# Six context tiles' values as three pairs of seven block products, with their sums on VectorE

## The chip, the cores and the metric

The kernel runs as one program on one core of one Trainium2 chip. The metric is the device time of one execution in microseconds (us). A core has a matrix engine (TensorE, "PE" in the profile, whose weight loads are "PEld"), VectorE ("DVE"), ScalarE ("ACT"), GpSimd ("POOL") and a queue engine (SyncE, "SP"), each with its own instruction stream; they wait for each other by semaphores. Matrix products read SBUF, the on-chip memory of 128 partitions, and are written to PSUM, eight banks of 2 KB a partition, here one tile of 128x512 float32 each.

## The reference, cut to what matters

Two layers work on a residual x of 2 x 256 tokens and 512 features. The first has an attention-like product with quantised factors and a mixture of experts; the second has a cross attention to 2 x 512 context rows, and then a low-rank layer with a gate. The cross attention, as the reference has it:

```python
q = (hidden_states @ q_proj_w.T).reshape(B, Q, NUM_HEADS, HEAD_DIM).transpose(0, 2, 1, 3)
k = (cross_attention_states @ k_proj_w.T).reshape(B, KV, NUM_KV_HEADS, HEAD_DIM)...
v = (cross_attention_states @ v_proj_w.T).reshape(B, KV, NUM_KV_HEADS, HEAD_DIM)...
q = rmsnorm(q, q_norm_w); k = rmsnorm(k, k_norm_w)
scores = einsum('bhqd,bhkd->bhqk', q, k) * scale + attention_mask
attn = softmax(scores); out = einsum('bhqk,bhkd->bhqd', attn, v)
return out @ o_proj_w.T
```

There are 32 query heads, 8 key and value heads ("groups" here, four query heads to each) and 128 features a head. The values of all groups are a matrix of 1024 context rows (8 tiles of 128) by 1024 columns, made from the context (512 features) and a weight matrix of 512 by 1024. The change is about the second half of its columns, groups 4 to 7.

## The kernel before, in words

All matrix products of this stage are float32. The values' first half is made at the start of the kernel. The second half is made at the start of the attention, by `values` (L723): for a context tile m, `context_product` (L216) multiplies four chunks of 128 features of the context, already transposed (`cT1`), with the weights `wv1` into one PSUM bank by four products of 128x512, and ACT copies the bank into `vv[:, m, 512:]` (L727).

The stage's order is written out at the end of the function, from L1100: layer norms of the four token tiles (L1103) and value tiles 0 and 1, the tokens turned (L1106), queries of group 0 for tiles 0 and 1, value tiles 2 and 3 (L1111), queries of tiles 2 and 3; then scores of unit (0, 0) two heads at a time (`probs`, L852) with a value tile behind each pair of heads: tiles 4, 5, 6, 7 at L1131, L1133, L1135, L1139. The first query products of group 1 stand between value tile 6 and the next scores (L1136). From L1141 a loop runs over units (group, token tile); it makes scores two units ahead, attends (`pav`), and makes queries and output products.

`in_order[0] = True` (L1101) holds PE's products and POOL's sums in the order in which the program writes them. DVE and ACT have no such order: the framework's planner places their instructions, each in one stream that runs strictly in order, and adds the semaphores. `tc.issue_after(x)` lets what is written inside be placed behind x.

Two other products of the stage already have a seven-product form (a product of 2x2 blocks by seven block products and sums of blocks, in the variant of Winograd). In `queries_begun` (L809) four block products of two steps of 128x256 are written into two banks `pe` and `po`; ACT copies one quarter to `u2`, and DVE forms three dependent adds (L824, L826, L827). In `queries_ended` (L830) three more block products accumulate into or overwrite quarters of the same banks, and DVE adds `u2` twice (L837, L838). The tiles `u2` and `u3` are in a pool with one buffer (`usum`, L718). Each query tile is normalised: ACT squares it (L735), DVE reduces it (L741, L743), POOL takes the root (L185), DVE multiplies (L748) and transposes blocks into `zq` (L231, one buffer), and 16 transfers turn `zq` into `qT` (L239), which the scores read. For groups after the first these transfers are issued by POOL.

A score tile (L863) lies in one of three PSUM buffers (`psa`). DVE adds the mask and finds the minimum (L871), ACT exponentiates (L876), DVE inverts the sum (L878), ACT scales (L879), DVE transposes blocks into `z` (L231), and SP moves `z` to `pT`.

`bank_of` (L74) hands out PSUM buffers from a list of pools in turn; the list `turns_b` is set by hand from stage to stage. `oT`, `zT`, the sums of heads (`head_sums`, L931) and the `shared` accumulators have SBUF buffers from the stage's start; two memsets on POOL clear `shared` (L1129).

## Time and profile before

Three runs took 636.58 us in the median (635.55 to 638.62). The profiled execution took 636.27 us, of which 634.5 us is the span between its first and its last recorded instruction.

| What | Value |
|---|---|
| profiled execution | 636.27 us, span 634.5 us |
| mean granted clock of TensorE | 0.997 |
| PE busy | 620.6 us, 98% of the span, 2013 instructions |
| DVE busy | 461.8 us, 73%, 1174 |
| ACT busy | 285.0 us, 45%, 567 |
| POOL busy | 302.1 us, 48%, 453 |
| value products of the second half (tiles 2 to 7) on PE | six tiles of 3.43 us each |
| ACT copy of a value tile (L727) | 0.58 us |

How to read it: a row of a timeline has the start in us, the length, the engine, the line of the kernel, the operation, output and input by the program's names, partitions and shapes, and the number of records merged; in brackets the idle time of the engine just before, and what ended it. PE records one float32 product as two records. The length of a merged PE row includes the draining of its last record, so the next row may start before it ends. DVE's instructions too are recorded with a small overlap. The granted clock is the share of full speed that the throttle let PE have.

### The profile page before, as it was taken

The page shows a single profiled execution, that of the slowest core. Times are in us where ns is not written, and L with a number is a line of the kernel's source. Part 1 is how long each engine was busy: PE and PEld are TensorE (multiplying, and loading weights), DVE is VectorE, ACT ScalarE, POOL GpSimd, SP SyncE. Part 2 cuts the span into 40 slices and gives each one's busy share as a digit, 9 for nine tenths or more (in the row PEclk, how much of TensorE's full clock was granted, in tenths as well). Part 3 has the DMA queues.
Part 4 walks back from the last instruction along what each step waited for, and adds up shares of the span by engine and source line. Part 5 has one row for each costly group of instructions (what it writes and reads, how often), then busy time and mean ns, then how long its engine had stood idle before and what let it go on. Part 6 is the DMA issues. An engine that isn't in the chain of part 4 may idle for free.

```text
span 634.5 us, 7774 instructions
## 1 busy us (share of the span) xinstructions
PE 620.6 (98%) x2013; PEld 395.9 (62%) x2013; DVE 461.8 (73%) x1174; ACT 285.0 (45%) x567; POOL 302.1 (48%) x453
## 2 busy tenths in 40 slices
PE   5999999999999999999999999999999999999997
PEld 2455345764456657776777767776677776665554
DVE  2568977765375888797887877878779788886533
ACT  0762132321165555555456545655555644644110
POOL 2308425301475772962844566467285346842200
PEclk9998999999999999999999999999999999999999
DMA  8740047450145754474474465457348446532101
GB/s 288 257 141 0 5 104 256 96 203 2 54 150 141 213 142 100 120 236 103 106 217 119 97 193 146 98 143 208 78 119 234 98 112 197 155 103 56 54 18 50
DMA packets 51950, 82.74 MB, mean 130 GB/s; under 512 B 15584, under 2 KB 17392, under 8 KB 51008
## 3 DMA queue, kind: packets, MB, share of 16 engines
q1 hardware_dynamic: 31232, 49.63, 28.3%
q10 hardware_dynamic: 11088, 19.41, 9.7%
q0 software_dynamic: 9584, 13.18, 7.7%
q8 instruction: 17, 0.28, 0.2%
q14 instruction: 29, 0.24, 0.1%
HBM read 34.97 MB, written 1.05 MB: 57 GB/s over the span
## 4 chain that ended last, share of the span: by engine, by line
PE 64%; DVE 0%; issue 0%; POOL 0%
PE pav L564 16%; PE px L564 16%; PE ps L564 15%; PE pq L564 11%; PE pz L564 2%; PE pout L564 2%; PE psc L564 1%; PE pzT L212 0%; PE pxn L212 0%; DVE qn L748 0%; DVE ot L1055 0%; POOL qrs L185 0%
## 5 line engine op out<-in xcount | busy, mean ns | idle before, releaser
L239 POOL DMA_DIRECT2D qT<-zq x232 | 114.4, 502 | 49.5 <-PE pav L564 32.3
L876 ACT ACTIVATE s<-s,nm 128x512 f32<-128x512 f32 x128 | 92.3, 721 | 75.4 <-DVE nm L871 69.3
L564 PE MATMUL ps<-kT,qT 128*128 128x512 f32 x256 | 121.0, 596 | 0.2 <-issue 0.2
L564 PE MATMUL pav<-pT,vv 128*128 128x512 f32 x256 | 115.3, 592 | 0.3 <-ACT s L879 0.3
L879 ACT ACTIVATE s<-s,rs 128x512 f32<-128x512 f32 x128 | 86.0, 710 | 55.2 <-DVE rs L878 42.6
L871 DVE CUSTOM_DVE_ANT_0 s<-ps,maskt 128x512 f32<-128x512 f32 x128 | 87.0, 681 | 24.1 <-PE ps L564 24.0
L231 DVE STREAM_TRANSPOSE z<-s 128x512 f32<-128x512 f32 x128 | 86.0, 697 | 14.6 <-ACT s L879 12.7
L564 PEld LDWEIGHTS ps<-kT,qT 128*128 128x128 f32 x256 | 77.9, 317 | 28.1 <-issue 4.5
L185 POOL TENSOR_TENSOR qrs<-qss,nhalf 128x4 f32<-128x4 f32 x32 | 32.3, 1015 | 103.9 <-DVE rs L878 59.4
L564 PEld LDWEIGHTS pav<-pT,vv 128*128 128x128 f32 x256 | 48.5, 190 | 49.9 <-issue 47.1
L221 PE MATMUL pk<-wk,cT 128*128 128x512 f32 x128 | 58.3, 611 | 1.1 <-DVE kn L291 1.1
L564 PE MATMUL pq<-wq,xnT 128*128 128x256 f32 (+1 forms) x200 | 57.4, 414 | 1.3 <-DVE qn L748 1.3
L564 PE MATMUL px<-wo,oT 128*128 128x256 f32 (+1 forms) x200 | 57.2, 413 | 0.0
L564 PEld LDWEIGHTS pq<-wq,xnT 128*128 128x128 f32 x200 | 37.7, 190 | 22.6 <-issue 16.1
L564 PEld LDWEIGHTS px<-wo,oT 128*128 128x128 f32 x200 | 37.8, 190 | 19.1 <-issue 12.7
L221 PEld LDWEIGHTS pk<-wk,cT 128*128 128x128 f32 x128 | 24.3, 195 | 30.2 <-issue 27.2
L221 PE MATMUL pv<-wv,cT 128*128 128x512 f32 x96 | 43.0, 593 | 0.2 <-PEq L689 0.2
L185 POOL TENSOR_TENSOR rs<-ve,nhalf 128x1 f32<-128x1 f32 x16 | 10.0, 629 | 64.5 <-DVE ve L196 50.0
L906 ACT COPY oT<-pav 128x512 f32<-128x512 f32 x32 | 18.4, 575 | 49.5 <-PE pav L564 49.5
L239 POOL DMA_DIRECT2D pT<-z x48 | 23.6, 499 | 32.9 <-issue 27.5
L878 DVE RECIPROCAL rs<-sm 128x1 f32<-128x1 f32 x128 | 19.4, 158 | 23.4 <-ACT s L876 22.1
L748 DVE TENSOR_TENSOR qn<-pq,qrs 128x512 f32<-128x512 f32 x32 | 22.1, 692 | 15.4 <-POOL qrs L185 15.4
(260 smaller groups left out, 937.1 us busy)
## 6 DMA issues: line engine op xcount, KB each, us to landing
pT<-z SPq DMA_DIRECT2D x464, 64.0 KB, 2.1
wo<-in_wqo_dram ACTq DMA_DIRECT2D x32, 256.0 KB, 3.9
qT<-zq POOLq DMA_DIRECT2D x232, 32.0 KB, 2.0
wq<-in_wqo_dram ACTq DMA_DIRECT2D x28, 256.0 KB, 3.9
kT<-vv SPq DMA_DIRECT2D x64, 64.0 KB, 2.0
cT<-in_cxT_dram SPq DMA_DIRECT2D x3, 1024.0 KB, 7.2
pT<-z POOLq DMA_DIRECT2D x48, 64.0 KB, 2.5
ct<-in_cx_dram SPq DMA_DIRECT2D x8, 256.0 KB, 4.7
```

Source lines behind the costliest of these rows:

```text
L185: last_root[0] = in_place(nc.gpsimd.tensor_tensor(dst, src, nhalf[:, :n], ALU.pow))
L221: last_product[0] = nc.tensor.matmul(ps, lhsT=c[:, kc, st * P : (st + 1) * P], rhs=w[:, kc, :], start=(kc == 0), stop=(kc == KC - 1),)
L231: nc.vector.transpose(z, src)
L239: ins = e.dma_start(dst[w * 32 : (w + 1) * 32, a], z[a * 32 : (a + 1) * 32, w])
L564: return in_place(nc.tensor.matmul(*args, **kw))
L748: nc.vector.tensor_tensor(qn, pq.rearrange("p (h d) -> p h d", d=HD), rq.unsqueeze(2).to_broadcast([P, REP, HD]), ALU.mult,)
L871: nc.vector.tensor_tensor_reduce(out=s, in0=sps, in1=maskt[:, mt, :], scale=-1.0, scalar=BIG, op0=ALU.add, op1=ALU.min, accum_out=nm,)
L876: nc.scalar.activation(s, s, AF.Exp, bias=nm, scale=-1.0, accum_out=sm)
L878: nc.vector.reciprocal(rs, sm)
L879: nc.scalar.mul(s, s, rs)
L906: nc.scalar.copy(oT.rearrange("p h a j -> p a h j"), po.rearrange("p (a h j) -> p a h j", a=NQ, h=REP),)
```

## The change

Value tiles 2 to 7 are made as pairs (2, 3), (4, 5), (6, 7). Each pair is a product of 256 context rows, 512 features and 512 columns. It is split into 2x2 blocks and made by seven block products of two steps of 128x256 each, in place of eight products of 128x512. Tiles 0 and 1 stay as they were.

- `value_weight_sums` forms four sums of blocks of `wv1` once, 128x512 each, and `value_sums` four sums of blocks of `cT1` for each pair, 128x256 each. All are DVE instructions. Some blocks are overwritten in place. Those of the weights and of pair 2 are written behind the last layer norm; those of pairs 4 and 6 behind the last add of pair 2.
- `values_begun` makes four of the seven products in two banks, has ACT copy a quarter to `u2` and DVE form three adds, the last into `vv`. `values_ended` makes the other three; ACT copies one quarter to `vv` and DVE adds twice into `vv`. `u2` and `u3` come from the pool `usum` with one buffer, by the tags that the queries use.
- In the order, `values_begun(2)` and `values_ended(2)` stand around the query product of tile 2. `values_begun(4)` and `values_ended(4)` stand where tiles 4 and 5 stood. `values_begun(6)` stands where tile 6 stood and `values_ended(6)` where tile 7 stood.
- The new sums have SBUF buffers in a pool at the right end of memory (`vsump`), closed behind `values_ended(6)`. The buffers of `oT`, `zT`, the heads' sums and `shared` are opened there then (`late`), and POOL's two memsets of `shared` move to that place.
- The list of PSUM buffers that the values use is set anew.

```diff
-        nc.vector.tensor_scalar(dst, src, mv[:, 0:1], rs, ALU.subtract, ALU.mult)
+        last_norm[0] = nc.vector.tensor_scalar(dst, src, mv[:, 0:1], rs, ALU.subtract, ALU.mult)
...
+        def value_weight_sums():
+            w = wv1.rearrange("p (i k) (j n) -> p i j k n", i=2, j=2)
+            b11, b12, b21, b22 = w[:, 0, 0], w[:, 0, 1], w[:, 1, 0], w[:, 1, 1]
+            t2, t3, t4 = (
+                vsump.tile([P, 2, 256], FP, tag=f"t{j}", bufs=1, name=f"vt{j}") for j in (2, 3, 4)
+            )
+            nc.vector.tensor_tensor(t3, b22, b12, ALU.subtract)
+            nc.vector.tensor_tensor(b12, b12, b11, ALU.subtract)
+            nc.vector.tensor_tensor(t2, b22, b12, ALU.subtract)
+            nc.vector.tensor_tensor(t4, b21, t2, ALU.subtract)
+            return b11, b21, b22, b12, t2, t3, t4
+
+        def value_sums(m):
+            b, st = divmod(m, S2 // P)
+            a = cT1[b].rearrange("p (i k) (s q) -> p i s k q", i=2, q=P)
+            a11, a12, a21, a22 = a[:, 0, st], a[:, 1, st], a[:, 0, st + 1], a[:, 1, st + 1]
+            s2, s3, s4 = (vsump.tile([P, 2, P], FP, tag=f"s{j}", name=f"vs{j}_{m}") for j in (2, 3, 4))
+            nc.vector.tensor_tensor(s3, a11, a21, ALU.subtract)
+            nc.vector.tensor_tensor(a21, a21, a22, ALU.add)
+            nc.vector.tensor_tensor(s2, a21, a11, ALU.subtract)
+            nc.vector.tensor_tensor(s4, a12, s2, ALU.subtract)
+            vsum_of[m] = a11, a12, a22, a21, s2, s3, s4
+
+        def values_begun(m):
+            a11, a12, a22, s1, s2, s3, s4 = vsum_of[m]
+            b11, b21, b22, t1, t2, t3, t4 = vsum_of["w"]
+            pe, po = (bank_of(turns_b, [P, 2, 256], FP, f"pv1_{m + o}") for o in range(2))
+            of_e = block_product(pe[:, 0], a11, b11, True)
+            of_o = block_product(po[:, 1], s2, t2, True)
+            with tc.issue_after(of_o):
+                block_product(po[:, 0], s3, t3)
+            with tc.issue_after(of_e):
+                block_product(pe[:, 1], s1, t1)
+            u2 = usum.tile([P, 256], FP, tag="u2", name=f"vu2_{m}")
+            nc.scalar.copy(u2, pe[:, 0])
+            nc.vector.tensor_tensor(u2, u2, po[:, 1], ALU.add)
+            u3 = usum.tile([P, 256], FP, tag="u3", name=f"vu3_{m}")
+            nc.vector.tensor_tensor(u3, u2, po[:, 0], ALU.add)
+            nc.vector.tensor_tensor(vv[:, m + 1, 768:], u3, pe[:, 1], ALU.add)
+            vpair_of[m] = pe, po, u2
+
+        def values_ended(m):
+            a11, a12, a22, s1, s2, s3, s4 = vsum_of.pop(m)
+            b11, b21, b22, t1, t2, t3, t4 = vsum_of["w"]
+            pe, po, u2 = vpair_of.pop(m)
+            block_product(pe[:, 0], a12, b21)
+            block_product(po[:, 0], a22, t4)
+            block_product(pe[:, 1], s4, b22)
+            nc.scalar.copy(vv[:, m, 512:768], pe[:, 0])
+            nc.vector.tensor_tensor(vv[:, m + 1, 512:768], u2, po[:, 0], ALU.add)
+            vpair_done[0] = nc.vector.tensor_tensor(vv[:, m, 768:], u2, pe[:, 1], ALU.add)
...
         for t in range(NT):
             turned(2, t)
-        turns_b[:] = [pso, pso, psb]
+        turns_b[:] = [pso]
         hold_loads[0] = True
+        with tc.issue_after(last_norm[0].ins):
+            vsum_of["w"] = value_weight_sums()
+            value_sums(2)
         next_queries(0)
         next_queries(1)
-        values((2, 3))
+        values_begun(2)
         next_queries(2)
         load_parts(4)
+        values_ended(2)
+        with tc.issue_after(vpair_done[0].ins):
+            value_sums(4)
+            value_sums(6)
...
-        for b in range(B):
-            nc.gpsimd.memset(shared[b], 0.0)
         probs(*units[0], (0, 1))
-        values((4,))
+        values_begun(4)
         probs(*units[0], (2, 3))
-        values((5,))
+        values_ended(4)
         probs(*units[1], (0, 1))
-        values((6,))
+        turns_b[:] = [psb, pso]
+        values_begun(6)
         next_queries(4)
         probs(*units[1], (2, 3))
+        values_ended(6)
         turns_b[:] = [pso]
-        values((7,))
+        vsums.close()
+        late.append(att.enter_context(tc.tile_pool(name="late", bufs=3, side="right")))
+        for b in range(B):
+            shared.append(late[0].tile([P, 2, 256], FP, tag=f"shared{b}", bufs=1, name=f"shared{b}"))
+            nc.gpsimd.memset(shared[b], 0.0)
```

More of the change, by code (lines that the diff above doesn't have):

```diff
@@ L188, in pool_sum @@
         in_place(nc.gpsimd.tensor_tensor(dst, a, b, op))
+    last_norm = [None]
     def layernorm(dst, src):
@@ L711, in tile_fq_moe_xattn_lora @@
         qtp = att.enter_context(tc.tile_pool(name="qtp", bufs=2))
-        opool = att.enter_context(tc.tile_pool(name="opool", bufs=3))
         spool = att.enter_context(tc.tile_pool(name="spool", bufs=4))
@@ L718, in tile_fq_moe_xattn_lora @@
         usum = att.enter_context(tc.tile_pool(name="usum", bufs=1))
+        vsums = ExitStack()
+        vsump = vsums.enter_context(tc.tile_pool(name="vsump", bufs=2, side="right"))
         norm_pool[:] = spool, "s"
@@ L729, in normed_queries @@
+        vsum_of, vpair_of, vpair_done = {}, {}, [None]
         def normed_queries(g, tiles, pqs):
@@ L904, in attend @@
             pT_of.pop((g, t))
-            oT = opool.tile([P, REP, NQ, 32], FP, tag="oT", name=f"oT{g}_{t}")
+            oT = late[0].tile([P, REP, NQ, 32], FP, tag="oT", name=f"oT{g}_{t}")
             nc.scalar.copy(
@@ L921, in project @@
             nc.vector.tensor_add(xs[t], xs[t], px)
-        shared = [
-            wsump.tile([P, 2, 256], FP, tag=f"shared{b}", name=f"shared{b}") for b in range(B)
-        ]
+        shared, late = [], []
         def head_sums(g, b):
@@ L934, in head_sums @@
             s2, s3, s4 = (
-                wsump.tile([P, 2, P], FP, tag=f"o{j}", name=f"o{j}_{g}_{b}") for j in (2, 3, 4)
+                late[0].tile([P, 2, P], FP, tag=f"o{j}", bufs=1, name=f"o{j}_{g}_{b}") for j in (2, 3, 4)
             )
@@ L1019, in gated_turned @@
         def gated_turned(t):
-            zT = opool.tile([P, KC, P], FP, tag="oT", name=f"zT{t}")
+            zT = late[0].tile([P, KC, P], FP, tag="oT", name=f"zT{t}")
             transposed(zT, f_of.pop(t).rearrange("p e r -> p (e r)"), f"pzT{t}")
```

## The prediction

> **What bounds the kernel now.** I read the page first, then the chain that ended last, then PE's waits, then the rows of PE, DVE, ACT and POOL from 150 to 232 us, where the change lies, and last the granted clock by windows. The first fence is the page (engine totals) and the chain's shares.

> ```profile
> PE 620.6 (98%) x2013; PEld 395.9 (62%) x2013; DVE 461.8 (73%) x1174; ACT 285.0 (45%) x567; POOL 302.1 (48%) x453
> PE 64%; DVE 0%; issue 0%; POOL 0%
> ```

> PE is the bound over the whole span; the chain is PE alone from 226 us to the end. So a PE slot removed is time removed, and a PE wait added is time added. PE's rows in the stage (start, length with drain, operation):

> ```profile
> 161.91 7.03 PE L221 MATMUL pv<-wv,cT 128*128 128x512 f32 x16
> 168.77 7.03 PE L564 MATMUL pq<-wq,xnT 128*128 128x512 f32 x16
> 175.64 1.88 PE L564 MATMUL ps<-kT,qT 128*128 128x512 f32 x4
> 177.36 3.60 PE L221 MATMUL pv<-wv,cT 128*128 128x512 f32 x8
> ...
> 191.09 1.03 PE L564 MATMUL pq<-wq,xnT 128*128 128x256 f32 x4
> 191.95 1.89 PE L564 MATMUL pq<-qt,xsum 128*128 128x256 f32 x8
> 193.68 1.03 PE L564 MATMUL pq<-wq,xnT 128*128 128x256 f32 x4
> ...
> 201.43 1.03 PE L564 MATMUL pq<-wq,xnT 128*128 128x256 f32 x4
> ```

> From 161.91 to 209 no row of PE shows a wait. The reader is to see two prices: a pair of value tiles takes 168.77 - 161.91 = 6.86 us, and the queries' products already have the new form: four block products 191.09 to 194.54 = 3.45, three 201.43 to 204.02 = 2.59. PE's waits of the span, in part:

> ```profile
> PE pv L309 <- DMA wv<-in_wkv_dram: 7.1, 1, 7.1
> PE pq L564 <- DVE qn L748: 1.3, 1, 1.3
> ```

> The 1.3 us stand at 226.36; behind that PE never stops for more than 0.3. Now DVE's rows where the new work goes:

> ```profile
> 183.32 1.30 DVE L231 STREAM_TRANSPOSE z<-s 128x512 f32<-128x512 f32 x2
> ...
> 195.15 0.42 DVE L824 TENSOR_TENSOR u<-u,pq 128x256 f32<-128x256 f32 x1 [3.77 <-ACT u L823]
> ...
> 229.63 0.40 DVE L937 TENSOR_TENSOR o<-oT,oT 128x256 f32<-128x256 f32 x1
> ```

> From 177.37 on DVE serves masks, transposes and normalisations with gaps of 0.1 to 0.8 us only. Last, the clock (columns: window; PE, PEld, DVE, ACT, POOL busy; PEclk; DMA share; GB/s):

> ```profile
> 52.40:55.90 3.50, 3.50 (x28) 3.02 (x27) 2.19 (x8) 1.57 (x7) 3.50 (x3) 1.00 0.00 0
> 55.90:59.30 3.40, 3.40 (x6) 1.49 (x6) 3.37 (x9) 0.89 (x3) 3.24 (x4) 0.50 0.00 0
> 59.30:62.70 3.40, 3.40 (x9) 1.52 (x8) 3.37 (x9) 0.47 (x1) 3.24 (x6) 1.00 0.00 0
> ```

> In the first window PE has mostly 16-column records and only two full ones of 128x512; then the clock is 0.50 for 3.4 us.

> **The change part by part.** Times are those of this trace.

> *PE, removed.* Three pairs at 3.45 + 2.59 = 6.04 instead of 6.86: 3 x 0.82 = 2.46 us less.

> *DVE, added.* Four sums of weights (128x512, pitch 0.61 by L748) and four of tiles 2, 3 (128x256; the head sums L937, L938 start 0.32 apart between SBUF operands): 2.4 + 1.3 = 3.8 us, placed behind the last layer norm, which ends at 153.96. They end near 157.8; DVE's next own work is the reduction at 159.35, and PE wants the sums at 162.8. Nothing. Eight more sums for tiles 4 to 7: 8 x 0.33 = 2.6 us. Five adds a pair, 15 in all; three of each pair form a dependent chain at 0.45 a step (195.15 to 195.60).

> *ACT.* Six copies of 128x512 (0.58) become six of 128x256 (0.37): nothing, ACT is 45% busy and waits for PE before most of them.

> *The new wait, first pair (2, 3).* The old products ended in one ACT copy and PE never waited. Now the second three products of a pair overwrite a bank that DVE must have read in its third add. Pair 2: first products end 165.4, the adds run behind the transpose at 165.7 and end 167.9; PE is on a query tile until 168.8. No wait.

> *Second pair (4, 5).* PE: three products end 171.4, query tile 174.8, two scores 176.5, four products 180.0, two scores 181.7. Then it wants DVE's third add. DVE's queue in the built order of the changed kernel: the query's product at 171.8 (square, reduction and POOL's root of 1.02 in front, 3.4 us before their old place), an add, 172.7; the transpose must wait for the reads of the same buffer by the transfers issued until 172 and landing 2.0 later, about 173.2; 0.95, an add 0.33, then the eight sums: 177.1. A reduction 0.61, mask 0.68, 0.08, mask 0.68: 179.1. The wait for POOL's root, as before (178.72 to 179.25): 179.6. Product 0.72, transpose 0.95, two masks with reciprocals 1.52, two transposes 1.26: 184.1. Three adds: 185.4. PE waits 185.4 - 181.7 = **3.7 us**. Everything on PE queues behind that wait: the tile's end, the next scores, and so their masks.

> *Third pair (6, 7).* Between its halves stand four query products and two scores, so its own adds (194.9 done) are early. But the query half-products use the same single-buffered "u2" tile: the ACT copy that stood at 194.74 must wait until DVE has read the values' u2 for the last time. PE: 185.4 + 2.6 + 1.7 + 3.5 + 3.45 + 1.7 = 198.4, three products to 201.0, two scores to 202.7; it then wants the query pair's third add. DVE's last value add ends 202.4 (behind two transposes), the copy 202.8, two masks are in front until 203.7, three adds: 205.0. PE waits **2.3 us**, where it waited nothing before.

> *What is late next.* At this point (201.43 before) PE stands at 205.1: 3.6 to 3.7 late = 3.7 + 2.3 - 2.4. From here a chain sets the wait at 226.36: the query tiles' products, POOL's 16 transfers (212.62 to 220.50), three sums, two roots, DVE's product. It shifts with PE. The small waits at 209.2 and 216.6 (0.1 and 0.3 us) vanish and the one at 226.36 grows by some 0.4, DVE having fewer leftovers in between: net **+3.3 us**.

> *POOL.* The two memsets (0.99) move from 139.95 behind the third pair, about 201; POOL is idle there from 198.8 to 207.4: nothing. SP's queue has the same transfers in the same order; ACT's loads of weights start up to 1.7 earlier or 2 us later, and are read at 220.5 by POOL: nothing.

> *The clock.* PE's 226.36 gap of 1.27 us left the clock at 1.00 (windows after it); the stretch before 55.90, with some 0.9 us of full records in 3.4, dropped it to 0.50 for 3.42 us; and after 7.07 us idle at the start records take 1061 ns instead of 592. A wait of 3.7 us is nearest to the second row: I take one drop, 3.42 / 2 = **+1.7 us**; bounds 0 and two drops, 3.4.

> [...]

> [...]

> **Sum.** The profiled execution took 636.27 us (span 634.5 and 1.8 around it); the median of the three runs shown is 636.58, 0.3 above. 636.27 + 3.3 + 1.7 = **641.3 us**.

> Unknowns: the sums of 128x256 at 0.33 each, up to 0.42 if their starts don't overlap (+0.7 on eight); the landing of the query transfers, 2.0 median and 3.7 at most in the trace (+1.7 on the first wait, since ACT's weight loads now start while they run); DVE 5% quicker than my rows would take 0.6 off. So without the clock +2.6 to +4.3 on most counts.

> **Rivals.**
> 1. *The clock stays at 1.00.* For it: the gap at 226.36 cost no clock. Against: that gap was a third as long. 636.27 + 3.3 = 639.6.
> 2. *Two drops.* Behind the 2.3 us wait too, or the first wait is a us or more longer by a late landing. For it: the stretch before 55.90 was not even idle. Against: 2.3 of 3.4 us leaves a third of a window busy. 636.27 + 3.3 + 3.4 = 643.0, with the landing 644.
> 3. *The waits are covered (other side).* If DVE reached the third add of the second pair by 181.7 and the u2 copy by 199, only the removed products would show: 636.27 - 2.46 = 633.8. The place is the eight sums and two transposes ahead of the add; it decides once DVE is there 3.7 us sooner, the sum of all eight sums and one and a half transposes. Against it: DVE has no gap from 173.2 to 179.1 in the built order and none from 179.6 to 185.4. Break-even needs both waits together under 2.5.

> **How the numbers follow.** One drop 0.52 (own range 640.3 to 642.5), no drop 0.27 (638.8 to 640.5), two drops or late landing 0.14 (642.5 to 644.8), covered waits in part or whole 0.07 (633.8 to 638.8). The range from 638.8 to 644.3 leaves out the last case and the end of the third. 0.5%, 3.2 us, is about what a measurement of this kernel can tell from no change: from 633.4 to 639.8 is "same": half of the second case (0.13) and most of the last (0.06); faster would need more than all that is removed: 0.02; slower 0.79.

> **What the profile after would show.** PE rows: pairs as 3.45 and 2.59 us (right), a wait near 181.7 of about 3.7 us put down to DVE's add into the values, one near 202.7 of about 2.3 us before the query products, and one near 229 of about 1.5 to 2. In windows of 3.4 us behind the first wait, a clock of 0.5. DVE: the eight sums in one block ahead of the reduction at 177. [...]

## The result

The changed kernel took 645.85 us in the median of four executions (642.73 to 649.1), the kernel before 637.34 us beside it: a ratio of 1.0141, 95% interval 1.0114 to 1.0168. The prediction was 641.3 us with a range of 638.8 to 644.3. The direction was right; the time lies above the range.

The profiled execution of after took 642.73 us, of which the span is 641.0. First the page: the engine totals and the chain's shares.

```profile
PE 618.1 (96%) x2049; PEld 402.8 (63%) x2049; DVE 471.9 (74%) x1205; ACT 283.6 (44%) x567; POOL 303.0 (47%) x453
PE 63%; DVE 0%; issue 0%; POOL 0%
```

PE is busy 2.5 us less than before, which is what the change takes away, and the span is 6.5 us longer all the same: PE waits. PE's rows of the stage (start, length, operation; in brackets the idle time in front and what ended it):

```profile
164.01 3.60 PE L566 MATMUL pq<-wq,xnT 128*128 128x512 f32 x8
167.45 1.03 PE L566 MATMUL pv<-wv,cT 128*128 128x256 f32 x4
...
170.04 3.60 PE L566 MATMUL pq<-wq,xnT 128*128 128x512 f32 x8
175.49 2.08 PE L566 MATMUL ps<-kT,qT 128*128 128x512 f32 x4 [1.86 <-DMA wq<-in_wqo_dram]
...
181.23 1.90 PE L566 MATMUL ps<-kT,qT 128*128 128x512 f32 x4
187.47 1.52 PE L566 MATMUL pv<-wv,cT 128*128 128x256 f32 x4 [4.34 <-ACT s L939]
...
208.85 1.10 PE L566 MATMUL pq<-wq,xnT 128*128 128x256 f32 x4 [2.16 <-DVE rs L938]
```

The second half of pair 2/3 takes 170.04 - 167.45 = 2.59 us, as priced. Then three waits follow that before has not: 1.86 us in front of the first scores, 4.34 in front of the second half of pair 4/5, 2.16 in front of the query half-products. The second and the third were predicted (3.7 and 2.3). The first was not. DVE's rows around the first two (the releaser that the 4.34 us are put down to, ACT's scaling, had long been done; the wait ends 0.15 after the third addition does):

```profile
175.39 1.12 DVE L233 STREAM_TRANSPOSE zq<-qn 128x512 f32<-128x512 f32 x1 [3.16 <-DMA wq<-in_wqo_dram]
...
176.69 0.73 DVE L752 TENSOR_TENSOR vs<-cT 128x256 f32<-128x256 f32 x2
...
179.34 0.68 DVE L801 TENSOR_REDUCE qss<-qn 128x4 f32<-128x512 f32 x1
...
186.90 0.42 DVE L773 TENSOR_TENSOR vv<-vu,pv 128x256 f32<-128x256 f32 x1
```

The eight sums take 179.34 - 176.69 = 2.65 us, the 2.6 of the prediction. But the block starts late: the transpose in front of it waits until 175.39, which is 176.7 in before's time (the stage starts 1.35 us earlier here), where the prediction had it start at about 173.2. Last the clock, by windows (columns: window; PE, PEld, DVE, ACT, POOL busy; PEclk; DMA share; GB/s):

```profile
184.61:188.02 3.41, 0.55 (x3) 0.53 (x4) 3.35 (x11) 3.35 (x8) 3.33 (x3) 1.00 0.20 51
188.02:191.43 3.41, 3.41 (x10) 2.70 (x9) 1.11 (x3) 0.00 (x0) 3.33 (x6) 0.50 0.34 79
```

One drop of the clock, 3.41 us at half speed behind the long wait, as predicted. So in this execution every predicted item is there. What makes its stage longer than predicted is the 1.86 us, 0.6 more on the first wait, and small change.

**A measure for the profiles.** The stage's first query product starts between 153.7 and 158.3 us in the profiles of this study, with nothing of the change ahead of it on PE; the late starts are those of executions with a clock drop near 70 us (loads_late, at half speed from 71.57 to 74.98, starts at 157.89). So profiles are compared from that product to the end of the span: before 634.5 - 155.04 = 479.5 us, after 641.0 - 153.69 = 487.3, **+7.8**, of which 1.7 is the drop (3.41 / 2). The prediction said +3.3 and +1.7, that is +5.0.

### The profile page after: what moved, and what is told of

It is laid out like the page before. It is cut to its first block, busy times and chain, and to the rows that moved or that the text cites. A ratio compares the mean times of both kernels' runs of the same rounds, so it can differ in the third digit from the quotient of the medians.

```text
span 641.0 us, 7884 instructions
## 1 busy us (share of the span) xinstructions
PE 618.1 (96%) x2049; PEld 402.8 (63%) x2049; DVE 471.9 (74%) x1205; ACT 283.6 (44%) x567; POOL 303.0 (47%) x453
## 4 chain that ended last, share of the span: by engine, by line
PE 63%; DVE 0%; issue 0%; POOL 0%
PE pav L566 16%; PE px L566 15%; PE ps L566 15%; PE pq L566 11%; PE pz L566 2%; PE pout L566 2%; PE psc L566 1%; PE pxn L214 0%; PE pzT L214 0%; DVE qn L808 0%; DVE ot L1113 0%; POOL qrs L185 0%
## 5 line engine op out<-in xcount | busy, mean ns | idle before, releaser
L223 PE MATMUL pk<-wk,cT 128*128 128x512 f32 x128 | 56.6, 596 | 2.0 <-DVE kn L293 2.0
L938 DVE RECIPROCAL rs<-sm 128x1 f32<-128x1 f32 x128 | 19.3, 157 | 23.1 <-ACT s L936 21.8
L233 DVE STREAM_TRANSPOSE zq<-qn 128x512 f32<-128x512 f32 x32 | 32.8, 1093 | 3.3 <-DMA wq<-in_wqo_dram 3.2
```

What stands on the lines that cost most here:

```text
L223: last_product[0] = nc.tensor.matmul(ps, lhsT=c[:, kc, st * P : (st + 1) * P], rhs=w[:, kc, :], start=(kc == 0), stop=(kc == KC - 1),)
L233: nc.vector.transpose(z, src)
L938: nc.vector.reciprocal(rs, sm)
```

## The experiments

The twelve runs, each beside executions of before on the same chip. "To the end" is the measure above, for the profiled execution; the mean clock is over all executions of the run.

| run | ratio to before (95%) | mean clock | to the end, us | half-speed windows from the stage's start to 240 us |
|---|---|---|---|---|
| after | 1.0141 (1.0114 to 1.0168) | 0.994 | 487.3 | 1 |
| after_again | 1.0135 (1.0108 to 1.0161) | 0.995 | 487.0 | 1 |
| loads_late | 1.0129 (1.0107 to 1.0151) | 0.991 | 487.5 | 3 |
| own_u2 | 1.0114 (1.0094 to 1.0134) | 0.993 | 485.6 | 1 |
| begun4_first | 1.0104 (1.0085 to 1.0124) | 0.994 | 485.1 | 1 |
| fill_wait | 1.0143 (1.0124 to 1.0161) | 0.996 | 486.6 | 1 |
| sums_gap | 1.0118 (1.0088 to 1.0148) | 0.993 | 483.5 | 0 |
| fill_own_u2 | 1.0052 (1.0030 to 1.0073) | 0.998 | 484.0 | 0 |
| before_less3 | 0.9981 (0.9963 to 0.9999) | 0.998 | 476.8 | 0 |
| all_four | 0.9984 (0.9968 to 1.0000) | 0.997 | 479.5 | 1 |
| four_two_queues | 0.9993 (0.9976 to 1.0009) | 0.998 | 478.1 | 0 |
| four_begun6 | 0.9996 (0.9977 to 1.0014) | 0.997 | 480.5 | 0 |
| before_two_queues | 1.0020 (1.0004 to 1.0037) | 0.997 | 479.8 | 0 |

Before itself has 479.5 and a mean clock of 0.998. One drop is 3.41 us at half speed, 1.7 of some 640 us, 0.0027 of the mean clock.

### Once more: the spread

> The kernel after once more, unchanged: a second profile, and how far its executions spread. In the profiles so far a drop of the granted clock takes 3.4 us (or 6.9) at half speed, 1.7 us of PE's work each (0.0027 of the mean clock); executions of before show 0.996 to 1.000, those of after 0.989 to 0.997, one to four drops. Theory T: waits at the same places as in the first profile (4.3, 2.2, 1.9, 1.1 us), and the times differ by the number of drops alone: 642.7 + 1.7 for each beyond the first, median 644.5 to 646. Rival: the waits themselves differ from execution to execution by microseconds.

Measured: 645.06 us in the median (642.96 to 647.99), waits of 4.3, 2.2, 1.6, 1.0, 0.5 and 0.2 us at the places of the first profile. The waits repeat; only the times and the mean clock spread. Of the ten executions of after taken together three have a mean clock of 0.997 (642.7 to 643.6), four of 0.995 (644.0 to 646.1), and the others 0.994, 0.991, 0.989 (647.0, 648.0, 649.1). None reaches 0.998 or more, which before often does.

### The loads of weights

```diff
         next_queries(2)
-        load_parts(4)
         values_ended(2)
...
         def first_sums():
+            load_parts(4)
             token_sums(False)
...
         next_queries(3)
-        wos[0] = weights_in_parts(wqo[0, 1], "wo0")
-        load_parts(4)
...
         probs(*units[0], (2, 3))
+        wos[0] = weights_in_parts(wqo[0, 1], "wo0")
+        hold_loads[0] = True
+        load_parts(4)
+        hold_loads[0] = False
```

(The sums of `wo0` on POOL move with its loads.)

> After, with ScalarE's four loads of wq1 behind the square of the fourth query tile (where those of wo0 stood) and wo0's four behind the exponentials of the first unit; every other engine keeps its order. In the profile of after wq1's loads are issued at 169.37 to 171.37, while the sixteen 32-KB transfers of the first unit's queries (issued 165.64 to 170.6) still land: the longest of these took 3.9 us to land (2.0 in the profile of before), and the first scores start at 175.49 with 1.86 us of wait that before has not. Theory T (the early loads hold the transfers up): the longest landing goes back to about 2 us, the 1.86 us of wait go, and the wait in front of the second half of pair 4/5 shrinks from 4.34 to about 3.7 because VectorE's transpose of the second unit's queries, now at 175.39, starts some 3 us earlier; 2.4 us less in all, 1.010 of before in place of 1.0141. Rival R (the transfers are late for another reason, their own issue or the queues' order): both waits stay, 1.014.

The time from issue to landing of the first unit's query transfers, for after and then for this run:

```profile
DMA to landing us min/median/max: 1.7/1.8/3.9
```

```profile
DMA to landing us min/median/max: 1.7/1.8/2.2
```

PE's waits of this run (what waited and for what; us in total, times, longest):

```profile
PE pv L566 <- ACT s L939: 4.2, 1, 4.2
PE pq L566 <- DVE rs L938: 2.2, 1, 2.2
PE ps L566 <- DVE qss L803: 0.9, 1, 0.9
```

The wait for the transfers is gone, the longest landing is 2.2 us: the loads of `wq1`, 4 x 256 KB, had held the last 32-KB transfers up (3.9 us to landing with the loads among them, 2.2 without). Their early start is a result of the change. In ScalarE's order they stand behind the square of the third query tile. In before that tile comes on PE behind both value tiles, in after between the halves of pair 2/3, so its square comes at 167.65 and not at 172.41, and the loads then wait only for the pair's second half to have read the buffer that they go into (its last product with `cT` ends at 169.34). They are issued at 169.37, 15.7 us behind the stage's first product, against 172.47 and 17.4 before. In before they follow the square's start by 0.06 us: there it was ScalarE's order, and not the buffer (the products with `cT` end at 168.94), that held them. By what way the loads slow the transfers, no run here shows.

The other half of the expectation failed: the first wait stayed at 4.2, for PE and VectorE moved forward together. VectorE's transpose still waits a little:

```profile
176.87 1.11 DVE L233 STREAM_TRANSPOSE zq<-qn 128x512 f32<-128x512 f32 x1 [0.44 <-DVE vv L784]
```

The addition to which the 0.44 us are put down had ended at 176.43. The last of the sixteen transfers was issued at 174.22 and landed 1.8 us later, at 176.06, and the transpose starts 0.8 behind that, as it starts 0.8 behind the last landing in sums_gap (178.04, 178.84) and begun4_first (178.88, 179.68). So the transfers set it here too.

And the ratio fell by 0.001 only, because this run's executions lost more clock (0.991): two windows in a row at half speed, 6.8 us, and a third drop, in the profile.

### The shared buffer

```diff
-            u2 = usum.tile([P, 256], FP, tag="u2", name=f"vu2_{m}")
+            u2 = vsump.tile([P, 256], FP, tag="vu2", bufs=1, name=f"vu2_{m}")
```

> After, with the values' copy of their first product in a buffer of its own, so that it no longer shares u2 with the query half-products. Theory T: the 2.16 us of wait in front of the query half-products at 208.85 go; the small waits that before has there (0.2 + 0.6 + 0.4) come back, so that PE ends 1.0 us earlier; 644.8, or 1.0125 of before; the first wait (4.34) and the 1.86 us stay. Rival: the wait is VectorE's own lateness behind the softmax and not the shared buffer: then it stays at about 2 us, and the ratio at 1.014.

```profile
PE pv L566 <- ACT s L939: 4.3, 1, 4.3
PE pq L566 <- DVE qn L808: 1.5, 2, 0.9
PE ps L566 <- DMA wq<-in_wqo_dram: 1.4, 1, 1.4
PE ps L566 <- issue: 0.6, 1, 0.6
```

The wait of 2.16 us is gone, and small waits come in its place, as expected: 2.1 us from there on, where after has 1.5 behind it. The shared buffer was its cause.

### The place of the pair's first half

```diff
-        probs(*units[0], (0, 1))
         values_begun(4)
+        probs(*units[0], (0, 1))
```

> After, with the first four products of pair 4/5 (and so their copy and their three additions in VectorE's order) in front of the first unit's scores of heads 0 and 1, in place of behind them. Theory T: the additions then stand ahead of the first softmax chain in VectorE's order, not behind it (the third addition at 186.90 is what PE waits 4.34 us for), so the wait falls under 1 us, which leaves nothing for the clock to drop on behind it (0.50 to 0.51 from 188.0 to 191.4 in the profile of after: 1.7 us), and the first scores, 3.4 us later in PE's order, find the query transfers landed (1.86 us). New: some 0.6 us of wait for the value sums in front of the pair. 4 + 1.9 + 1.7 - 0.6 - 1 (small waits that come back): some 5 us off 642.7, so 637 to 639, 1.001 to 1.004 of before. Rival R1 (VectorE's added load, some 30 additions of 0.33 to 0.42 us, is the cause, wherever they stand): the wait moves behind the next scores and the time stays above 642.

PE's wait did not go but moved, inside the pair:

```profile
178.04 1.03 PE L566 MATMUL pv<-wv,cT 128*128 128x256 f32 x4
182.84 3.36 PE L566 MATMUL pv<-vt,vs 128*128 128x256 f32 x8 [3.77 <-DVE vs L754]
```

and VectorE's rows say why:

```profile
179.68 1.10 DVE L233 STREAM_TRANSPOSE zq<-qn 128x512 f32<-128x512 f32 x1 [2.88 <-DMA wq<-in_wqo_dram]
180.63 0.40 DVE L785 TENSOR_TENSOR vv<-vu,pv 128x256 f32<-128x256 f32 x1
180.96 0.73 DVE L752 TENSOR_TENSOR vs<-cT 128x256 f32<-128x256 f32 x2
```

The value sums stand behind the pair's last addition, this one behind the transpose, and the transpose waits for the transfers. It is neither the theory's path nor the rival's (added load): one late transfer holds VectorE's whole queue. So the ratio of 1.0104 missed the 1.001 to 1.004 expected; that the time, 643.06 us, is above the rival's 642 does not make the rival's cause right.

### Filling the first wait

```diff
         probs(*units[0], (2, 3))
+        pf = psb.tile([P, 512], FP, tag="b", name="pfill")
+        for k in range(4):
+            product(pf, lhsT=xnT[:, 0, :P], rhs=wqs[0][:, 0, :], start=(k == 0), stop=(k == 3))
         values_ended(4)
```

> After, with four products of 512 columns (0.86 us each) that nobody reads in a free PSUM bank, in front of the second half of pair 4/5: PE works through 3.4 of the 4.34 us of its wait, and nothing else is changed. If the low clock behind that wait comes from PE's idling, as the prediction has it, the drop at 188 is gone, and with it 1.7 us: 641.0 for an execution without other drops, 1.0115 of before over all. If the drop has another cause (the additions' or the transfers' activity), it stays at 0.50 for 3.4 us, and the time with it.

The planner also placed the loads of `wo0` later on ScalarE. The wait for the transfers is 0.9 us here, but 1.4 in fill_own_u2 with the same placing, as in own_u2 without it; so this wait differs between the profiles (0.9 to 1.9), and the placing isn't shown to matter. The drop at 188 is gone. But another stands behind the second wait, of 2.16 us (windows as above):

```profile
184.78:188.19 3.41, 2.50 (x8) 1.09 (x7) 3.35 (x10) 3.37 (x8) 3.33 (x3) 1.00 0.20 51
...
205.26:208.67 3.41, 1.33 (x6) 1.23 (x7) 3.04 (x11) 2.81 (x6) 0.00 (x0) 1.00 0.68 197
208.67:212.08 3.41, 3.41 (x8) 2.38 (x8) 1.11 (x3) 0.08 (x1) 0.00 (x0) 0.50 0.98 270
```

A window in which PE worked for 1.33 of 3.41 us was followed by one at half speed. The ratio of 1.0143 missed the 1.0115 expected: three of the four executions still had two drops by their mean clock (0.995). PE's idling as the cause is supported by the drop that went, but the run by itself does not settle it.

### The sums in VectorE's gap

```diff
         values_begun(2)
+        with tc.issue_after(vpair_mid[0].ins):
+            value_sums(4)
+            value_sums(6)
         next_queries(2)
...
-        with tc.issue_after(vpair_done[0].ins):
-            value_sums(4)
-            value_sums(6)
```

(`vpair_mid` holds the third addition of the pair.)

> After, with the eight value sums of pairs 4/5 and 6/7 (2.65 us on VectorE, 176.69 to 179.34 in the profile of after) directly behind the third addition of pair 2/3, where VectorE idles from 166.72 to 168.28, in place of behind the pair's last addition. Theory T (the sums stand in the stretch that VectorE works through without a pause, from the late transpose at 175.39 to the third addition at 186.90, and so in PE's wait one for one): 1.6 to 2.6 us off the first wait, 4.3 to between 1.7 and 2.7; a walk through the queues with the durations of the trace and transfers that land in time gives only 0.3, since the chain of the first softmax (scores, table load 1.28, exponential, transpose) then ends last; both are worked out beforehand, and what is measured chooses. The 1.86 us of the transfers may change as well, since VectorE's work on the third query tile moves by up to 1.1 us.

```profile
PE pv L566 <- DVE vv L773: 3.3, 1, 3.3
PE pq L566 <- DVE rs L938: 2.2, 1, 2.2
PE pq L566 <- DVE qn L808: 1.2, 1, 1.2
PE ps L566 <- DMA wq<-in_wqo_dram: 1.0, 1, 1.0
```

The first wait fell by 1.0 us, between the two calculations. But that is the difference of two moves. Seven of the eight sums went into the gap (the planner left one behind the transpose, at 179.81), and counted from the stage's first product the third addition ends 2.2 us earlier than in after (31.4 for 33.6 us). PE arrives 1.2 us earlier as well, most of it because the wait in front of the scores is 1.0 in place of 1.86 us here. So VectorE gained nearly the seven sums' price, as the theory has it. In front of the additions there remain the transpose, which waits for the transfers until 178.84, and the chain of the first softmax. And behind the wait of 3.32 us the clock stayed at 1.00 here; the wait lies across a border of windows, and PE was busy for 1.94 and 1.57 us in the two:

```profile
184.24:187.66 3.42, 1.94 (x5) 1.01 (x4) 2.77 (x9) 2.61 (x6) 3.34 (x3) 1.00 0.12 31
187.66:191.07 3.41, 1.57 (x7) 1.44 (x8) 2.97 (x8) 2.22 (x6) 3.25 (x4) 1.00 0.21 52
```

Other executions of the same kernel did pay: the six have a mean clock of 1.000 once (640.45 us, the fastest), 0.997 (the profiled one), 0.992 and three times 0.989.

### What the removed products are worth

```diff
-    def context_product(c, w, m, name, bank=None):
+    def context_product(c, w, m, name, bank=None, n=KC):
...
-        for kc in range(KC):
+        for kc in range(n):
```

(with n = 3 for the value tiles 2, 4 and 6 in before)

> Before, with the last of the four products of 512 columns left out for the value tiles 2, 4 and 6: their last quarter of features isn't summed (this part of the computation is left out, which doesn't matter to the time of the rest). That is three products of 0.858 us, 2.57 us, what the change takes off PE's queue (2.46 by the prediction), with nothing added to any engine. Theory T: the time falls by about as much, 633.9, 0.996 of before: the removed products are worth their price, and what after loses is the waits. Rival (PE's time there is covered by VectorE's chain or by the transfers): the time stays within 0.7 us of before.

In the profile the stage ends 479.5 - 476.8 = 2.7 us earlier, for 2.57 us removed. Over twelve executions the ratio is 0.9981, 1.2 us, with an interval (0.1 to 2.4 us) that does not quite reach the price. So the products stand on PE's path in the profile; how much of them an average execution keeps is not settled by this run, since the interval also holds times that the rival allows (at most 0.7 us).

### The four moves together

> After with the four moves together: ScalarE's loads of wq1 and wo0 later (as in loads_late), the eight sums in VectorE's gap (sums_gap), pair 4/5 begun in front of the first scores (begun4_first), and the values' u2 in a buffer of its own (own_u2). Theory T: the three PE waits of after that stand before 210 (4.3, 2.2, 1.9 us) all fall under 1 us and no drop of the clock is left in this stage; what stays are waits of about 1.1 us (query halves) and up to 2.4 us on the transfers of the second probabilities. By the walk PE ends 1.4 us ahead of before: 635, 0.998 (0.996 to 1.001). Rival: VectorE is the bound of the stage, whatever the order; then the waits turn up again behind the next additions and the time stays above 639.

Its edit is that of loads_late, sums_gap, begun4_first and own_u2. PE's waits behind 145 us are these two alone:

```profile
PE pav L566 <- DMA pT<-z: 2.2, 1, 2.2
PE pq L566 <- DVE qn L808: 0.9, 1, 0.9
```

All three new waits are gone and the ratio is 0.9984, within what was expected and 1.5% under after. The rival (VectorE is full, whatever the order) falls. But the products' 2.46 us do not come out: PE now arrives early at the products that read unit 1's probabilities, waits 2.18 us for their transfers, and pays a drop behind it:

```profile
211.77:215.18 3.41, 1.23 (x4) 0.44 (x3) 3.16 (x11) 2.17 (x6) 3.30 (x7) 1.00 0.73 206
215.18:218.59 3.41, 3.41 (x4) 1.48 (x5) 1.32 (x2) 0.86 (x2) 3.29 (x7) 0.50 0.65 167
```

### The next wait

```diff
-                [nc.sync, nc.gpsimd] if (g, t) >= (NKV - 2, 2) else [nc.sync],
+                [nc.sync, nc.gpsimd] if (g, t) >= (NKV - 2, 2) or (g, t) == (0, 1) else [nc.sync],
```

> all_four, with the sixteen transfers of unit 1's probabilities (pT of the second tile) on SyncE's and GpSimd's queues by turns, where all stood in SyncE's, one behind the other at some 0.6 us each. In the profile of all_four PE waits 2.18 us for them at 215.18, and the clock falls to 0.50 right behind, from 215.2 to 218.6; before the four moves PE came later and waited for nothing there. Theory T (what the four moves win is given back to these transfers): the wait falls under 0.6 us; some 1 us of it comes back at the wait for the queries behind (0.9 us at 207.5, none at 226 in all_four), the drop behind it goes in most executions: 0.995 of before (0.992 to 0.999). Rival (the transfers' landing, not their issue, is what is late): the wait stays, 0.998 as all_four.

> Before, with the transfers of unit 1's probabilities on two queues, and nothing else. PE waits for them nowhere in the profile of before (0.0 at the products that read them, its only waits behind 155 are 1.3, 0.3, 0.2 and 0.2 us), so the theory expects the same time as before, within 0.2%: what four_two_queues gains beyond all_four is then the removed products' price and no gain of its own. Rival: the second queue is a gain by itself, 0.997 or less.

> four_two_queues, with pair 6/7 begun in front of the scores of unit 1's heads 0 and 1 as pair 4/5 is in front of unit 0's. Its additions then stand further ahead of the query half-products, whose wait in all_four's profile is 0.88 us at 207.5. By the walk PE ends 1.2 us ahead of four_two_queues: 0.994 of before. Rival (VectorE is full there): no gain on four_two_queues, and a wait of over 1 us in front of the second half of pair 6/7.

With two queues the wait for the probabilities is gone and the stage has no drop; what PE waits for is this:

```profile
PE pq L566 <- DVE qn L808: 1.9, 2, 1.0
PE ps L566 <- issue: 0.2, 1, 0.2
```

To the end it takes 478.1 us, 1.4 less than before. Over its twelve executions the ratio is 0.9993, not the 0.995 expected, and not to be told from before. The same edit in before gives 1.0020: no gain by itself, rather a small loss. The two kernels with two queues, run on one chip, can be compared with each other: 636.3 us against 638.1 in the mean of twelve executions each, 1.8 us (95%: 0.5 to 3.0) for the form with seven products, so a part of the products' 2.46 us does come out. Pair 6/7 begun earlier as well (its edit is that of begun4_first for the next pair) brings a wait of 3.06 us at the first products with probabilities, by the profile put down to a DMA, and nothing on the whole (0.9996, where 0.994 was expected); its cause stays open. So the form with seven products can be brought level with before, and no version here beats before as it was by more than 0.2%, which is within what the measurement can tell from no change.

### Both waits taken from the clock

The edit is that of fill_wait and own_u2 together.

> fill_wait and own_u2 together: four products that nobody reads fill 3.4 us of the first wait, and the buffer of its own takes the second wait away; the work of the change is all there. (The planner also puts ScalarE's loads of wo0 behind the first exponentials here, as in fill_wait.) In the seven profiles of after and its variants so far, each drop of the clock in this stage followed a window of 3.41 us in which PE was busy for 0.00 to 1.33 us, and none followed windows with 1.57 us or more. Theory T, clock part (a window with less than some 40% of PE's work makes the next one run at half speed): no window of this stage falls under 1.5 us, so the profile shows no drop from 160 to 240, the mean clock over the executions rises from 0.993 to 0.996 (after and its variants) to that of before, 0.998, and the time is that of the waits alone: 1.007 to 1.009 of before. Rival (the drops have another cause, such as the additions' or the transfers' load): drops as in fill_wait and own_u2, mean clock 0.993 to 0.996, 1.011 to 1.014.

Measured: 640.98 us, 1.0052 of before (1.0030 to 1.0073). No drop from the stage's start to 240 us, where PE is busy for 2.05 us or more in each window; the mean clock over the executions is 0.998, as before's (0.997 beside it). Against own_u2 only idle time of PE was filled, with work that nobody reads, and (by the planner) four loads moved; the time is 0.006 of 637, some 4 us, shorter, and the difference of the mean clocks (0.9983 against 0.9927) makes 3.6 of it. The moved loads alone don't do it: loads_late moves them too, and has three drops. A part may be chance, since executions also lose windows ahead of the stage (the profiled one has a mean clock of 0.997, with no drop in the stage); but that PE's idling lowers the clock here, and that the clock is microseconds of after's loss, is shown by this run and not only argued. The expectation for the time (1.007 to 1.009) was too high.

## Why the prediction was wrong

**Right.** The price of the removed products (3.45 and 2.59 us a pair in the rows of after). The sums' price (2.65 for 2.6). The second wait by place, size and cause: 2.16 for 2.3 us, and it goes when the buffer isn't shared. The first wait by place and cause (the third addition, behind the first softmax on VectorE). The waits behind 226 us: 1.5 us in all (0.4 at 230.2 and 1.1 at 233.4), at the low end of what was expected. POOL's memsets and the sums of the weights cost nothing.

**The step that failed: "ACT's loads of weights start up to 1.7 earlier ... nothing".** The start was read rightly (1.75 us earlier, counted from the stage's first product) and its cost was set at nothing, though the paragraph on the unknowns names the same collision as up to 1.7 us on the first wait. It cost 1.86 us in front of the scores, before that wait, and nothing on the wait itself: in loads_late the 1.86 us go and the 4.2 stay. A landing of 2.0 us, the median over the whole trace, was taken for the last of sixteen transfers; the last one is what PE and VectorE wait for, and the longest landing became 3.9.

**The first wait, 4.34 for 3.7.** The term that was too small is the start of the transpose. The prediction's own figures, issue until 172 and landing 2.0 later, make 174.0 and not the 173.2 that it went on with. In loads_late, where the early loads are away, the transpose starts 18.98 us behind the stage's first product; that is 174.0 in before's time, and the wait is 4.2. In after it starts later still, behind the late transfers, but PE arrives later too. POOL is not what decided it. The root of the third query tile does start late, at 170.15, right behind the eight transfers that POOL issues until 170.13, and VectorE waits 2.04 us for it, where the first two tiles' roots take 1.13; the prediction had no queue in front of it. But in front of the transpose VectorE then idles all the same, for 3.16 us in after and 0.44 in loads_late. This is read from rows; no run moved the transfers' issue by itself.

**The clock: one drop, +1.7.** The profiled execution has exactly that, but it is a mild one. In the profiles a drop goes with the window of 3.41 us before it: here are PE's busy times in that window, for the seven profiles with a drop behind one of the stage's waits: 0.00, 0.00, 0.23, 0.53, 0.55 us (waits of 3.8 to 4.3 us), and 1.23, 1.25, 1.33 us (waits of 2.2). Windows with 1.57, 1.61 and 1.94 us were followed by full speed. These are windows with full-size products. The row before 55.90 that the prediction leans on shows PE busy for all of its 3.50 us, mostly with products of 16 columns, and the clock fell all the same, so busy time isn't the whole measure. So rival 2 was argued away by a wrong sentence: "2.3 of 3.4 us leaves a third of a window busy" speaks for a drop, not against it. The second wait cost one too where it fell well into a window (1.33 us of work in fill_wait, 1.25 in loads_late), and the first cost two in loads_late (187.62 to 194.45). The mean clock, 0.9945 over ten executions of after against 0.998 of before, is 0.0035 x 645 = 2.3 us on average, and up to four drops in the slowest. So one drop was too few for an average execution. Rival 2 had the mechanism; its price, 643 to 644, is still below the median, and it was given 14%.

**The sum.** To the end of the profiled executions: products -2.5, waits 4.3 + 2.2 + 1.9, the small waits behind 209 us 1.5 where before has 1.8, so -0.3, one drop 1.7, together 7.3 of the 7.8 measured. No run traced the rest, 0.5. About as much stands in PE's rows right behind the wait of 1.86 us: from 175.49 to 181.23 they take 5.74 us, and the same rows of loads_late, which has no wait there, 5.17 (177.67 to 182.84). The medians stand 8.5 apart, more than the profiles, since the profiled execution was the fastest of its four: the other three have a mean clock of 0.995, 0.995 and 0.989 for its 0.997.

**A reading.** "From 177.37 on DVE serves masks, transposes and normalisations with gaps of 0.1 to 0.8 us only" holds until 191.4; behind that the row at 195.15, shown with it, has a gap of 3.77 us. The first wait lies ahead of it, so nothing came of that.

**The chances.** 0.79 on slower was right, and the range was too narrow: its upper end held two drops or a late landing, and they came together. The profiled execution, with one drop, took 642.73 us, inside the range; it is the clock of the other executions that puts the median above it.

## What to carry to other kernels

When a change moves forward the instruction behind which a load stands in an engine's order, the load starts earlier too (here by 1.75 us, though no buffer came free earlier); ask which small transfers, already under way, it will meet, and cost the last of them, not the median one (3.9 and 1.8 us here). A wait on PE had a second price here, the clock: in this stage it fell behind windows of 3.41 us in which PE was busy for 0.00 to 1.33 us, so a wait of 2.2 us could cost 1.7 more, and the same kernel spread from 642.7 to 649.1 us. And a product that is taken off the bounding engine only pays if what it waited behind keeps up: here, with the three new waits gone, PE met the next transfer (2.18 us in all_four).

## What the runs showed of the hardware

```profile
187.62:191.03 3.41, 2.10 (x5) 1.77 (x6) 2.49 (x7) 1.81 (x4) 3.25 (x3) 0.50 0.46 121
191.03:194.45 3.42, 3.42 (x9) 2.71 (x9) 0.42 (x1) 0.02 (x1) 3.42 (x8) 0.50 0.99 276
```

  The stage's other low windows, with 2.82 us and more at half speed, were all followed by full speed, and one far ahead of the stage, with 2.65 us (begun4_first, from 69.61), was not. Counted as work at full speed, 1.33 is too little and 1.41 enough. That is near the bounds above, 1.45 and 1.57, but does not quite meet them; the measure is not known to a tenth.
- In eight of the fourteen profiles, that of before among them, the clock drops near 55 or 70 us (before from 55.90, loads_late from 71.57), far ahead of the change; the starts of the changed stage lie 4.6 us apart. Two single profiles can differ by that with no change at all.
